# The end of an attention-and-density kernel: pacing of the last norm, early diagonals, order of the last units, a halved ending

## The chip, the cores and the metric

The kernel runs on one core of a Trainium2 chip. The core has a matrix engine (TensorE, PE in the profile, with its weight loads as PEld), a vector engine (VectorE, DVE), a scalar engine for activation functions (ScalarE, ACT), a general engine (GpSimd, POOL) and a queue for transfers (SyncE, SP). Each engine runs its own instructions in order and waits on semaphores for the others. The metric is the device time of one execution in microseconds (us). All data is float32.

## The reference

Two layers run one after the other on x of shape (8, 192, 64, 64). Cut to what matters:

```python
# layer 0: attention over the 4096 pixels of each image
x = x + L0(_gn(x))     # q, k: 24 channels, v: 192; out = softmax(q k) v
# layer 1: a density per value, with small per-channel matrices
def _logits_cumulative(logits, ms, bs, fs):         # filters 1, 3, 3, 3, 1
    for i in range(4):
        logits = einsum('cij,cjn->cin', softplus(ms[i]), logits) + bs[i]
        if i < 3:
            logits = logits + tanh(fs[i]) * tanh(logits)
    return logits
lower = _logits_cumulative(xr - 0.5, ms, bs, fs)    # xr = _gn(x)
upper = _logits_cumulative(xr + 0.5, ms, bs, fs)
sign = -sign(lower + upper)
likelihood = maximum(abs(sigmoid(sign * upper) - sigmoid(sign * lower)), 1e-06)
x = x + likelihood
```

`_gn` is a group norm over an image: a mean and a variance for each group of six channels. The density of an image can thus not start before the whole image has its attention result and the norm of that result is known.

## The kernel before, in words

The attention is one long stream of 1024 steps, 128 for each of the 8 images (`last = B * IMG`). A step multiplies queries and keys into scores (L769, PE), takes their exponential (L773, ACT) and multiplies it with the values (L784, PE). Row maxima for the softmax run 22 steps ahead (L697 on PE, L705 on DVE). Everything else is put between these by a small planner that works while the program is written, not while it runs.

The planner has two parts. `at(t, fn, cost, act, pe)` files a function under a step; `work_off(t, rate)` writes out what is due at that step, then starts a waiting PSUM job, then calls `density_step`. This second part deals out the density work of the image before: it gives each engine a credit per step (for DVE and PE the `rate`, for ACT 2.9 during the stream and the `rate` after it), and lets the oldest three units write out instructions while the credit lasts. A function that is filed with a cost takes its cost from the credit. So after the stream, where `t` no longer stands for a piece of attention, the `rate` says how many us of density work are written between two steps of anything else. It is 4.15.

A density unit is one of 12 pieces of an image: half c, channel group g, and s for lower or upper; its tiles are 128 x 1024. It goes through three rows of three: a tanh of x (L994), a linear part of x (L1003), nine multiply-adds ("mix", L1026), then gates and further affine steps and additions (L1019 and L1009 on ACT, L1026 on DVE). A `Unit` of the last image other than its first one takes its first nine multiply-adds and the linear part to PE instead: three sums of four products with diagonal matrices (`product`, L967), one diagonal per coefficient; its tanh of a sum is L975 and its gate L985. There are eleven such units. When lower and upper of a piece are both done, `ending` adds them, takes two tanhs, subtracts, masks, takes the absolute value and adds to x, and stores the result by two transfers (L1202). After the stream this is the form `alone`, on DVE and ACT.

The diagonals lie in freed tiles of the values. `diagonals(g)` makes nine for a group by scaling an identity on ACT (L865); it is filed for the fifth to seventh step after the stream. `linear_diagonals` (L871) makes the three that need the last norm, for all three groups, then works out the offsets `lower2` on DVE (L877 to L883), and hands four PSUM tiles to the units (`banks`): the two accumulators `b`, and `sc_tail` and `mx_tail`.

The end of the last image's attention is a chain of planner steps: a reciprocal (L804), two evacuations on ACT (L808), six transposes on PE (L817), the residual addition (L826), three statistics (L427), an aggregate (L436), a group mean on PE (L441), differences (L447 to L451), a group variance on PE (L456), L462 and L463, a square root on ACT (L469), and the final small steps (L475 to L491), which write `wn` and `bn`, the scale and offsets of the norm. Each of these stands in a step of its own, some thirteen in all. Then `density(7)` adds the 12 units of the last image. When only two units are left, the one with more DVE work goes first.

Of the kernel before, what the change touches and what calls it, by code (L numbers as in the profile page):

```python
# [10 lines left out]
AF = mybir.ActivationFunctionType  # L11
ALU = mybir.AluOpType
# [5 lines left out]
def kernel(  # L18
# [40 lines left out]
    nc = tc.nc  # L59

    B, C, H, W = x.shape
    N = H * W
    CR = w1t.shape[1]
    F = 512
# [4 lines left out]
    R = C // 3  # L69
# [4 lines left out]
    last = B * IMG  # L74
# [95 lines left out]
    for s in range(2):  # L170
        p = slice(R * s, R * s + R)
# [684 lines left out]
    banks = deque()  # L856
    lower2 = mm.rearrange("p g n -> p (g n)")[:, 0:36].rearrange("p (s g i) -> p s g i", s=4, g=3)

    def diagonals(g):

        d = vtiles.pop(0).rearrange("p a b c -> p (a b c)")[:, 0 : 12 * 128]
        d = d.rearrange("p (k n) -> p k n", k=12)
        diag.append(d)
        for k in range(9):
            nc.scalar.activation(d[:, k, :], ident, AF.Copy, scale=lc[:, g, k : k + 1])  # L865

    def linear_diagonals(b):
        wn, bn = norms[b, 1]
        for g in range(3):
            for i in range(3):  # L870
                nc.scalar.activation(  # L871
                    diag[g][:, 9 + i, :], ident, AF.Copy, scale=wn[:, g, 1, i : i + 1]
                )

        for s in range(2):
            d, q = lower2[:, s], lower2[:, 2 + s]
            nc.vector.tensor_copy(d, cb[:, :, 6:9])  # L877
            for j in range(3):
                nc.vector.tensor_tensor(
                    q, wsp[:, :, 12 + j : 21 : 3],  # L880
                    bn[:, s, :, 1, j : j + 1].to_broadcast([128, 3, 3]), ALU.mult,
                )
                nc.vector.tensor_tensor(d, d, q, ALU.add)  # L883
        for t in (
            *turns, ps_sc.tile([128, 2, F], F32, tag="sc", name="sc_tail"),
            ps_mx.tile([128, 2, F], F32, tag="mx", name="mx_tail"),
        ):
            banks.append(t)
# [186 lines left out]
    def density_step(t, rate):  # L1075
        if units and t < last:

            left = sum(len(u.todo["DVE"]) for u in units if u.key[0] == units[0].key[0])
            rate = left * COST["DVE"] / max(1, (units[0].key[0] + 2) * IMG + 15 - t) + OTHER
        act = ACT_RATE if t < last else rate  # L1080

        for eng, most in (("DVE", rate), ("ACT", act)):
            more = (rate if eng == "DVE" else 0.0) if t >= last else 1.3
            credit[eng] = min(credit[eng] + most, most + more)
        credit["PE"] = min(credit["PE"] + rate, rate)
        for eng in ("ACT", "PE", "DVE"):
            order = list(range(min(3, len(units))))
            if len(units) == 2:

                order.sort(key=lambda n: -len(units[n].todo["DVE"]))  # L1090
            for n in order:
                units[n].step(eng, t, list(units)[:n])
        for u in [u for u in units if not u.todo["DVE"]]:
            units.remove(u)

    def density(b):
        if b == B - 1:
            linear_diagonals(b)
# [25 lines left out]
    def ending(b, c, g):  # L1124


        z = [zs.pop((b, c, g, i)) for i in range(2)]
        halves = [slice(h * F, h * F + F) for h in range(2)]
        cell = {}

        def later(n, fn, *cost):
            at(now[0] + n, fn, *cost)

        def begin():
            if not bufs:
                later(1, begin)
                return
            endings.pop()
            cell["s"] = bufs.pop(0)
            if now[0] < last - 12:  # L1140
                for h in range(2):
                    pieces.append(lambda h=h: total(h))
            else:
                alone()

        def total(h):
            n = halves[h]
            later(1, lambda: tanhs(h), 0.0, 2.0)
            return nc.gpsimd.tensor_tensor(cell["s"][:, n], z[0][:, n], z[1][:, n], ALU.add)  # L1149

        def tanhs(h):
            for i in range(2):
                nc.scalar.activation(z[i][:, halves[h]], z[i][:, halves[h]], AF.Tanh, scale=0.5)
            s = cell["s"][:, halves[h]]
            nc.scalar.activation(s, s, AF.Sign)
            pieces.append(lambda: difference(h))
            pieces.append(lambda: masked(h))

        def difference(h):
            n = halves[h]  # L1160
            return nc.gpsimd.tensor_tensor(z[0][:, n], z[1][:, n], z[0][:, n], ALU.subtract)  # L1161

        def masked(h):
            n = halves[h]
            if h == 1:
                later(1, lambda: bufs.extend((cell["s"], z[1])))
                later(1, size, 0.0, 1.1)
                later(2, store, 1.3)
            return nc.gpsimd.tensor_tensor(z[0][:, n], z[0][:, n], cell["s"][:, n], ALU.mult)  # L1169

        def alone():

            s = cell["s"]

            def first():
                nc.vector.tensor_tensor(s, z[0], z[1], ALU.add)
                later(1, second, 0.0, 2.1)

            def second():
                for i in range(2):  # L1180
                    nc.scalar.activation(z[i], z[i], AF.Tanh, scale=0.5)
                later(1, third, 2.5)

            def third():
                nc.vector.tensor_tensor(z[0], z[1], z[0], ALU.subtract)
                nc.vector.scalar_tensor_tensor(z[0], s, 0.0, z[0], ALU.not_equal, ALU.mult)
                bufs.extend((s, z[1]))
                later(1, size, 0.0, 1.1)
                later(2, store, 1.3)

            later(1, first, 1.25)

        def size():
            nc.scalar.activation(z[0], z[0], AF.Abs, scale=0.5)

        def store():
            x_ = xc[b, c][:, g, :]
            nc.vector.scalar_tensor_tensor(x_, z[0], 1e-6, x_, ALU.max, ALU.add)
            bufs.append(z[0])
            for i in range(2):  # L1200
                k = i * N // 2 + c * 2 * F
                nc.sync.dma_start(  # L1202
                    out=ov[b, :, g, k : k + 2 * F], in_=x_[R * i : R * i + R]
                )
# [55 lines left out]
    def prepare(b, t):  # L1260
        seen = []

        def then():
            seen.append(0)
            if len(seen) == NP:
                norm_end((b, 0), 2 * NP, now[0] + 1, lambda: weights(b, normed))

        def normed():
            for i, c in enumerate(ORDER):
                for h in range(2):  # L1270
                    what = "kv" if i < 2 else "k"
                    use(b, 2 * c + h, what, max(now[0], t + 30 + 6 * (2 * i + h)), 1, 0, i < 2)

            for h in range(2):
                use(b, h, "q", t + 92, 0, 1, 0, t + 97)

        for d in range(NP):
            look(b, d, t + 1 + d, then)

        for i in (2, 3):  # L1280
            for h in range(2):
                use(b, 2 * ORDER[i] + h, "v", t + 100 + 4 * i + 2 * h, 0, 0, 1, t + 107 + 4 * i)
        for h in range(2):
            use(b, 2 + h, "q", t + 122, 0, 1, 0, t + IMG)
# [86 lines left out]
    for g in range(3):  # L1371
# [5 lines left out]

# [36 lines left out]
```

## Time and profile before

| What | Value |
|---|---|
| Median of 3 runs | 4918.28 us (4916.8 to 4919.44) |
| Profiled execution | 4916.79 us, span 4915.0 us |
| PE busy | 4740.1 us, 96% of the span |
| DVE busy | 4312.6 us, 88% |
| ACT busy | 3194.5 us, 65% |
| POOL busy | 514.0 us, 10% |
| Mean granted TensorE clock | 0.987 |
| Last attention matmul of the stream ends | about 4552 us |
| Norm results of the last image (L488) | 4603.25 us |
| First matmul of a PE unit that reads a tanh | 4615.66 us |
| Last matmul of a PE unit ends | about 4878.6 us |
| Last store instruction ends | about 4910.3 us |

The span runs from the first to the last instruction; the execution's own time is 1.79 us more. Times of single instructions below are counted from the span's start. A row of the order of time merges equal instructions that follow each other: its second number is their busy time together, and the number in brackets is the time for which the engine was idle before it, with the engine and line that ended the wait. The recorded duration of a DVE or ACT instruction overlaps the next one's by about 0.1 us. A matmul of a PE unit is two rows of 512 columns.

### The profile page before, as it was taken

To read this page: it belongs to the slowest core of one execution; us is meant where nothing else is said; L and a number is where in the kernel's file an instruction comes from. 1 tells how busy PE (TensorE), PEld (TensorE's weight loads), DVE (VectorE), ACT (ScalarE), POOL (GpSimd) and SP (SyncE) were. 2 spreads that over 40 slices of the span, in tenths; PEclk is the share of its full clock that TensorE was granted. 3 is DMA by queue.
4 is the path that set the end of the run, shared out by engine and by line. 5 is a ranking of instruction groups with operands and counts; after the bars stand their busy time and mean duration, and the time that the engine had idled before them with its cause. 6 is when DMAs were issued, how large, how long until landed. Compare 5 with 4: busy or idle time off the path is not lost.

```text
span 4915.0 us, 69887 instructions
## 1 busy us (share of the span) xinstructions
PE 4740.1 (96%) x29152; PEld 3505.3 (71%) x29152; DVE 4312.6 (88%) x4442; ACT 3194.5 (65%) x3709; POOL 514.0 (10%) x506
## 2 busy tenths in 40 slices
PE   7999999999999999999999999999999999999496
PEld 5777777777777777777777777777777777777232
DVE  5433359999999999999999999999999999998987
ACT  2333347776767766776776767776767767676765
POOL 0000001111011110210111200111111111111000
PEclk9999999999999999999999999999999999999798
DMA  2000020111200111010110111011111101000000
GB/s 56 26 22 18 14 52 4 32 28 31 51 18 18 42 37 34 23 37 24 42 30 21 32 40 40 18 31 32 31 34 32 28 22 28 11 22 5 9 13 13
DMA packets 111953, 135.49 MB, mean 28 GB/s; under 512 B 14738, under 2 KB 93076, under 8 KB 111636
## 3 DMA queue, kind: packets, MB, share of 16 engines
q1 hardware_dynamic: 110432, 130.65, 10.9%
q8 instruction: 228, 3.74, 0.3%
q14 instruction: 89, 0.73, 0.1%
q10 hardware_dynamic: 1204, 0.37, 0.0%
HBM read 105.82 MB, written 25.17 MB: 27 GB/s over the span
## 4 chain that ended last, share of the span: by engine, by line
PE 78%; DVE 16%; ACT 4%; issue 1%; POOL 1%; DMA 0%; ACTq 0%; SPq 0%; DVEq 0%; POOLq 0%
PE b L784 46%; PE sc L769 18%; DVE d L1026 10%; DVE rm L705 4%; PE b L658 4%; PE b L967 2%; PE b L630 2%; PE b L601 1%; PE sc_tail L967 1%; PE mx_tail L967 1%; PE mx L697 1%; PE b L817 1%; ACT d L1019 1%; ACT d L1009 1%; ACT e L773 1%
## 5 line engine op out<-in xcount | busy, mean ns | idle before, releaser
L784 PEld LDWEIGHTS b<-v,e 128*128 128x128 f32 x16384 | 2655.1, 190 | 777.0 <-issue 772.5
L784 PE MATMUL b<-v,e 128*128 128x193 f32 x16384 | 2958.9, 334 | 0.0
L773 ACT ACTIVATE e<-sc 128x1024 f32<-128x1024 f32 x1024 | 1046.7, 1022 | 1456.3 <-PE mx L697 1414.0
L705 DVE TENSOR_REDUCE rm<-mx 128x1 f32<-128x1024 f32 x1002 | 1223.3, 1221 | 459.6 <-PE mx L697 454.2
L769 PE MATMUL sc<-q,k 25*128 25x512 f32 x4096 | 1155.2, 640 | 16.8 <-ACT e L773 16.4
L697 PE MATMUL mx<-k,q 24*128 24x512 f32 x4008 | 1130.4, 640 | 4.9 <-DVE rm L705 4.9
L1026 DVE SCALAR_TENSOR_TENSOR d<-d,wsp,d 128x1024 f32<-128x1024 f32 x768 | 988.0, 1288 | 44.3 <-ACT d L1019 33.6
L1026 DVE SCALAR_TENSOR_TENSOR d<-d,lc,d 128x1024 f32<-128x1024 f32 x765 | 981.6, 1291 | 18.1 <-ACT d L1003 5.1
L1026 DVE SCALAR_TENSOR_TENSOR d<-d,tf,d 128x1024 f32<-128x1024 f32 x543 | 683.9, 1280 | 3.5 <-ACT d L1009 3.4
L1009 ACT ACTIVATE d<-d 128x1024 f32<-128x1024 f32 x543 | 569.6, 1055 | 57.1 <-DVE d L1026 55.7
L769 PEld LDWEIGHTS sc<-q,k 25*128 25x128 f32 x4096 | 306.2, 182 | 250.2 <-issue 195.8
L1114 POOL MEMSET pause<- 128x1 f32 x240 | 23.7, 99 | 3965.9 <-DVE d L1026 3965.9
L1019 ACT ACTIVATE d<-d,cb,wsp 128x1024 f32<-128x1024 f32 x351 | 433.3, 1235 | 0.8 <-DVE d L1026 0.2
L994 ACT ACTIVATE d<-xc,bn,wn 128x1024 f32<-128x1024 f32 x288 | 354.1, 1236 | 2.8 <-DVE bn L491 2.0
L1003 ACT ACTIVATE d<-xc,bn,wn 128x1024 f32<-128x1024 f32 x255 | 315.7, 1238 | 0.0
L697 PEld LDWEIGHTS mx<-k,q 24*128 24x128 f32 x4008 | 299.6, 182 | 16.9 <-DVE rm L705 13.5
L1149 POOL TENSOR_TENSOR d<-d,d 128x512 f32<-128x512 f32 x80 | 169.5, 2119 | 0.2
L1161 POOL TENSOR_TENSOR d<-d,d 128x512 f32<-128x512 f32 x80 | 167.7, 2097 | 0.0
L1169 POOL TENSOR_TENSOR d<-d,d 128x512 f32<-128x512 f32 x80 | 156.4, 1955 | 2.3 <-POOL pause L1114 0.6
L658 PE MATMUL b<-wv,xi 64*128 64x192 f32 x1344 | 139.5, 340 | 1.4 <-ACT pra L585 1.4
L658 PEld LDWEIGHTS b<-wv,xi 64*128 64x128 f32 x1344 | 106.5, 186 | 26.9 <-issue 20.9
L967 PE MATMUL b<-d,v 128*128 128x512 f32 x204 | 95.2, 618 | 17.0 <-ACT d L994 17.0
(171 smaller groups left out, 2373.5 us busy)
## 6 DMA issues: line engine op xcount, KB each, us to landing
xi<-in_x_dram SPq DMA_DIRECT2D x392, 192.0 KB, 3.4
xc<-in_x_dram SPq DMA_DIRECT2D x64, 384.0 KB, 8.0
out_dram<-xc SPq DMA_DIRECT2D x96, 256.0 KB, 3.2
d<-in_x_dram SPq DMA_DIRECT2D x16, 192.0 KB, 4.0
d<-in_wat_dram ACTq DMA_DIRECT2D x2, 144.0 KB
cb<-in_den_b_dram SPq DMA_DIRECT2D x6, 2.2 KB, 2.1
ff<-in_den_f_dram SPq DMA_DIRECT2D x6, 2.2 KB, 2.2
bq<-in_b_dram ACTq DMA_DIRECT2D x4, 0.1 KB
```

Of the source, the lines that this page charges most:

```text
L658: nc.tensor.matmul(pv[:, s, 0:C], lhsT=t[p, g, k * 128 : k * 128 + 128] if g < 3 else one_row[p], rhs=wf["v", b][p, g, :] if g < 3 else wf ...
L697: nc.tensor.matmul(sc[:, s, :], lhsT=tile_of(qt[b, n // 2], n, j)[r], rhs=kt[b][r, u : u + F], start=True, stop=True,)
L705: nc.vector.tensor_reduce(out=rowmax[b, n][:, j, k : k + 1], in_=sc, axis=AX.XY, op=ALU.max)
L769: nc.tensor.matmul(sc[:, s, :], lhsT=kt[b][r, k : k + 128], rhs=qt[b, n // 2][r, :, u : u + 256], start=True, stop=True,)
L773: return lambda: nc.scalar.activation(e, sc, AF.Exp)
L784: nc.tensor.matmul(a[:, j, 0 : C + 1], lhsT=e[:, s, j * 128 : j * 128 + 128], rhs=v[:, s, p % 4, :], start=p == 0 and s == 0 and j % 2 == ...
L967: nc.tensor.matmul(out[:, h, :], lhsT=diag[g][:, 3 * i + n - 1 if n else 9 + i, :], rhs=src[:, h * F : h * F + F], start=n == 0, stop=n == 3,)
L994: nc.scalar.activation(self.buf[k], self.src(), AF.Tanh, bias=bn[:, s, g, 0, i : i + 1], scale=wn[:, g, 0, i : i + 1],)
L1003: nc.scalar.activation(self.buf[k], self.src(), AF.Identity, bias=bn[:, s, g, 1, i : i + 1], scale=wn[:, g, 1, i : i + 1],)
L1009: nc.scalar.activation(self.buf[k], self.buf["l", k[1], k[2]], AF.Tanh)
L1019: nc.scalar.activation(self.buf[k], self.buf["l", n - 1, 0], AF.Identity, bias=offset, scale=wsp[:, g, w : w + 1],)
L1026: nc.vector.scalar_tensor_tensor(dst, src, factor, dst, ALU.mult, ALU.add)
```

## The change

Four things change, all behind or near the end of the stream.

- After the stream the `rate` is 1.3 instead of 4.15 until the last norm's results are there, and 4.15 from then on. Fewer density instructions are written between the steps of the norm's chain.
- The 27 diagonals that don't need the norm are made during the last image, one per planner step, at steps 93 to 101, 104 to 112 and 117 to 125 of its 128. Each is filed with 0.4 of ACT.
- The three diagonals that need the norm are made at once for group 0, three steps later for group 1 and six steps later for group 2. The offsets and the hand-over of the PSUM tiles (`tail`) come one step later than the norm, with a DVE cost of 2.2.
- After the stream the last two units keep their order, older first. The very last ending is written in two halves of 512 columns, with four transfers instead of two.

```diff
-    def diagonals(g):
+    def diagonals(g, t):
+        def one(k):
+            if k == 0:
+                d = vtiles.pop(0).rearrange("p a b c -> p (a b c)")[:, 0 : 12 * 128]
+                diag.append(d.rearrange("p (k n) -> p k n", k=12))
+            nc.scalar.activation(diag[g][:, k, :], ident, AF.Copy, scale=lc[:, g, k : k + 1])
-        d = vtiles.pop(0).rearrange("p a b c -> p (a b c)")[:, 0 : 12 * 128]
-        d = d.rearrange("p (k n) -> p k n", k=12)
-        diag.append(d)
         for k in range(9):
-            nc.scalar.activation(d[:, k, :], ident, AF.Copy, scale=lc[:, g, k : k + 1])
+            at(t + k, lambda k=k: one(k), 0.0, 0.4)
...
-            if len(units) == 2:
+            if len(units) == 2 and t < last:
                 order.sort(key=lambda n: -len(units[n].todo["DVE"]))
...
         if b == B - 1:
-            linear_diagonals(b)
+            linear_diagonals(b, 0)
+            for g in (1, 2):
+                at(now[0] + 3 * g, lambda g=g: linear_diagonals(b, g), 0.0, 1.2)
+            at(now[0] + 1, lambda: tail(b), 2.2)
...
             s = cell["s"]
+            parts = halves if (b, c, g) == (B - 1, 1, 2) else [slice(0, 2 * F)]
             def first():
-                nc.vector.tensor_tensor(s, z[0], z[1], ALU.add)
+                for n in parts:
+                    nc.vector.tensor_tensor(s[:, n], z[0][:, n], z[1][:, n], ALU.add)
                 later(1, second, 0.0, 2.1)
             def second():
+                for n in parts:
+                    for i in range(2):
+                        nc.scalar.activation(z[i][:, n], z[i][:, n], AF.Tanh, scale=0.5)
...
+            for n in parts:
+                x_ = xc[b, c][:, g, n]
+                nc.vector.scalar_tensor_tensor(x_, z[0][:, n], 1e-6, x_, ALU.max, ALU.add)
                 for i in range(2):
...
+                        out=ov[b, :, g, k + n.start : k + n.stop], in_=x_[R * i : R * i + R]
...
             if b + 1 < B:
                 prepare(b + 1, t)
+            else:
+                diagonals(0, t + 93)
+                diagonals(1, t + 104)
+                diagonals(2, last - 11)
...
-    for g in range(3):
-        at(t + 4 + g, lambda g=g: diagonals(g))
     while due or units or jobs or loads:
-        work_off(t, RATE)
+        work_off(t, RATE if (B - 1, 1) in norms else 1.3)
         t += 1
```

More of the change, by code (lines that the diff above doesn't have):

```diff
@@ L857, with linear_diagonals, tail @@
     lower2 = mm.rearrange("p g n -> p (g n)")[:, 0:36].rearrange("p (s g i) -> p s g i", s=4, g=3)
-    def diagonals(g):
-        d = vtiles.pop(0).rearrange("p a b c -> p (a b c)")[:, 0 : 12 * 128]
-        d = d.rearrange("p (k n) -> p k n", k=12)
-        diag.append(d)
+    def diagonals(g, t):
[4 more added lines that the diff above has]
+            nc.scalar.activation(diag[g][:, k, :], ident, AF.Copy, scale=lc[:, g, k : k + 1])
         for k in range(9):
-            nc.scalar.activation(d[:, k, :], ident, AF.Copy, scale=lc[:, g, k : k + 1])
-    def linear_diagonals(b):
+            at(t + k, lambda k=k: one(k), 0.0, 0.4)
+    def linear_diagonals(b, g):
         wn, bn = norms[b, 1]
-        for g in range(3):
[L870 to L873, printed above, removed]
+        for i in range(3):
+            nc.scalar.activation(
+                diag[g][:, 9 + i, :], ident, AF.Copy, scale=wn[:, g, 1, i : i + 1]
+            )
+    def tail(b):
+        wn, bn = norms[b, 1]
         for s in range(2):
@@ L1173, in alone @@
             s = cell["s"]
+            parts = halves if (b, c, g) == (B - 1, 1, 2) else [slice(0, 2 * F)]
             def first():
-                nc.vector.tensor_tensor(s, z[0], z[1], ALU.add)
+                for n in parts:
+                    nc.vector.tensor_tensor(s[:, n], z[0][:, n], z[1][:, n], ALU.add)
                 later(1, second, 0.0, 2.1)
             def second():
-                for i in range(2):
-                    nc.scalar.activation(z[i], z[i], AF.Tanh, scale=0.5)
+                for n in parts:
+                    for i in range(2):
+                        nc.scalar.activation(z[i][:, n], z[i][:, n], AF.Tanh, scale=0.5)
@@ L1182, in second @@
                 later(1, third, 2.5)
             def third():
-                nc.vector.tensor_tensor(z[0], z[1], z[0], ALU.subtract)
-                nc.vector.scalar_tensor_tensor(z[0], s, 0.0, z[0], ALU.not_equal, ALU.mult)
+                for n in parts:
+                    y = z[0][:, n]
+                    nc.vector.tensor_tensor(y, z[1][:, n], y, ALU.subtract)
+                    nc.vector.scalar_tensor_tensor(y, s[:, n], 0.0, y, ALU.not_equal, ALU.mult)
                 bufs.extend((s, z[1]))
-                later(1, size, 0.0, 1.1)
@@ L1189, in third, with size @@
-                later(2, store, 1.3)
+                later(1, lambda: size(parts), 0.0, 1.1)
+                later(2, lambda: store(parts), 1.3)
             later(1, first, 1.25)
[L1193 to L1198, printed above, removed]
-            bufs.append(z[0])
[L1200 to L1204, printed above, removed]
+        def size(parts=(slice(0, 2 * F),)):
+            for n in parts:
+                nc.scalar.activation(z[0][:, n], z[0][:, n], AF.Abs, scale=0.5)
@@ L1205, in store @@
+        def store(parts=(slice(0, 2 * F),)):
+            for n in parts:
+                x_ = xc[b, c][:, g, n]
+                nc.vector.scalar_tensor_tensor(x_, z[0][:, n], 1e-6, x_, ALU.max, ALU.add)
+                for i in range(2):
+                    k = i * N // 2 + c * 2 * F
+                    nc.sync.dma_start(
+                        out=ov[b, :, g, k + n.start : k + n.stop], in_=x_[R * i : R * i + R]
+                    )
+            bufs.append(z[0])
             if g == 2:
@@ L1370 @@
     homes[:] = [(turns[1], [0, 0])]
-    for g in range(3):
-        at(t + 4 + g, lambda g=g: diagonals(g))
     while due or units or jobs or loads:
-        work_off(t, RATE)
+        work_off(t, RATE if (B - 1, 1) in norms else 1.3)
         t += 1
```

## The prediction

> **What bounds the kernel now.** I read the stage table first, then each engine's instructions in order of time, then the waits. The table below gives five stretches: start:end and length, then busy time with the instruction count for PE, PEld, DVE, ACT and POOL, the granted TensorE clock, and the DMA share.
>
> ```profile
> 4400.00:4551.00 151.00, 150.51 (x852) 113.46 (x851) 136.00 (x123) 107.57 (x113) 14.01 (x13) 1.00 0.08 18
> 4551.00:4604.00 53.00, 3.67 (x17) 2.80 (x15) 51.08 (x62) 34.58 (x58) 0.00 (x0) 0.56 0.04 10
> 4604.00:4716.00 112.00, 87.39 (x183) 37.23 (x184) 90.42 (x85) 74.65 (x75) 0.00 (x0) 0.87 0.04 10
> 4716.00:4871.00 155.00, 142.58 (x329) 61.74 (x328) 132.24 (x108) 104.99 (x98) 0.00 (x0) 1.00 0.04 10
> 4871.00:4915.00 44.00, 7.63 (x18) 3.04 (x16) 30.75 (x25) 18.20 (x17) 0.00 (x0) 0.62 0.09 24
> ```
>
> The stream ends near 4552. In it PE is the bound (150.51 of 151). In the next 53 us PE does almost nothing while DVE is full (51.08): DVE works on image 6's last units, with the last norm's small steps between them. From 4616 the PE units run; in their settled part (third stretch from the end to 4871) PE is busy 92%. The last 44 us are one unit's DVE and ACT chain.
>
> ```profile
> 4569.10 0.95 DVE L826 TENSOR_TENSOR xc<-xc,b 128x768 f32<-128x768 f32 x1
> 4603.25 0.23 DVE L488 TENSOR_SCALAR wn<-wx,nrm 128x18 f32<-128x18 f32 x1
> 4615.66 6.88 PE L967 MATMUL b<-d,v 128*128 128x512 f32 x12 [7.91 <-ACT d L994]
> 4639.80 1.98 PE L967 MATMUL mx_tail<-d,v 128*128 128x512 f32 x4 [1.81 <-ACT d L994]
> 4652.85 5.34 PE L967 MATMUL mx_tail<-d,v 128*128 128x512 f32 x8 [11.06 <-ACT d L994]
> ...
> 4698.07 8.34 PE L967 MATMUL b<-d,v 128*128 128x512 f32 x12 [3.83 <-ACT d L994]
> ...
> 4746.28 5.42 PE L967 MATMUL mx_tail<-d,v 128*128 128x512 f32 x12 [1.81 <-ACT d L994]
> ```
>
> Columns: start, busy, engine, line, operation, count; in brackets the idle time before it and who ended it. The norm's results (L488) come 51 us after the stream. The first PE unit starts at 4615.66; its successor waits 11.06 in the middle of a sum and the next 3.83, because the tanh inputs (L994) stand in ACT's queue behind DVE work. Later each unit waits only about 1.8.
>
> **The change, part by part.**
>
> *Short steps.* Between the reciprocal at 4551.97 and the norm's first reciprocal at 4602.20, DVE runs 37 wide instructions. In the new order there are 11: five before the residual, none up to the statistics' end, two, two and two between the three later small groups. I lay them out with the old rows: 1.20 between independent wide instructions, 1.31 when one needs its predecessor, 1.13 an ACT affine, 0.96 a tanh, 0.05 a handoff. The ending of image 6's unit waits once for its absolute value on ACT, so the residual starts at 4560.9 (was 4569.10), the aggregate ends at 4563.4, the mean is read at 4565.9, the variance at 4569.5, the norm's reciprocal starts at 4572.1. The norm is 30.1 us earlier.
>
> But the 26 displaced instructions do not vanish. The planner lets only the oldest three units step, so image 6's last two units and the one non-PE unit of image 7 go ahead of the first PE unit. Between the lower2 work and the first PE gate DVE now has 47 wide instructions (was 16). From 4575.9, 33 at 1.20 and 14 dependent ones at 1.31 give 58; with one 0.7 us wait for an ACT affine and 1.2 for another, the first gate comes at 4635.7, later than the old 4629.24. The first PE unit's tanh inputs stand behind the 33rd of these: they finish at 4619.8, 4621.0 and 4625.75, so PE starts 4.1 us later than 4615.66. So the early norm alone gains nothing at this point: at about 4616 DVE has done the same number of instructions in both orders, since it was nearly full.
>
> What it gains comes after. The non-PE unit is then further along, and PE's 11.06 and 3.83 waits fall away. First sum done 4628.0 (third input, two matmuls of it, 0.5 for a slow start); then ten sums at 6.87 and three unit waits of 1.75 put the eleventh at 4702.0. In the old trace the eleventh sum ends at 4713.3. Lead: 11.3. From about the eleventh gate the DVE order is the old one, and ACT's nearly so, so the lead carries on: the settled cycle (45.3 per two units) is unchanged.
>
> A wait of 3.83 before 4698.07 was followed by 12 matmuls in 8.34 instead of 5.42: 2.9 lost at half clock, part of what is saved. The Trainium skill ("TensorE: Matmul & The Clock Gate", What's actually happening) has the half clock return after an idle window of about 3.4 us. The 1.8 rows show no slowing. Here the page speaks against the change in one place: PE is now idle from 4559 and starts with three broken-up inputs. By the page 3.4 us of work at half rate would cost 1.7; the wait for the third input covers all but about 0.5, which I take. By the row of the old start (6.88 for 12, against 5.16 at the 0.43 pace) it would also be 1.7: range 0 to 1.7.
>
> *Diagonals in the stream.* 27 ACT copies leave the gap for the last image, one a step.
>
> ```profile
> 4424.12 1.00 ACT L773 ACTIVATE e<-sc 128x1024 f32<-128x1024 f32 x1
> 4519.52 1.02 ACT L773 ACTIVATE e<-sc 128x1024 f32<-128x1024 f32 x1 [2.84 <-PE sc L769]
> 4565.65 7.99 ACT L865 ACTIVATE v<-ident,lc 128x128 f32<-128x128 f32 x27
> 4595.89 1.28 ACT L469 ACT_TABLE_LOAD   x1
> 4597.18 0.20 ACT L469 ACTIVATE sq<-ve 128x1 f32<-128x1 f32 x1
> ```
>
> Each costs 0.30 (7.99/27). In most steps ACT idles 0.6 to 2.8 before the next exponential and hides it. In about two of the 27 steps ACT is already late (no idle, as at 4424.12) and queued behind the copy is the exponential, then the attention matmuls. Bounds: 0, and 27 x 0.30 = 8.0 if every step passed it on. I take two steps, 0.5. In the gap their removal saves nothing, since DVE was the bound there.
>
> *Table loads.* Two stay, before the square root and before the next tanh, but the second now stands before image 6's tanh. The Trainium skill ("ScalarE: Activation LUTs", What ACT_TABLE_LOAD costs) charges 1.28 plus a drain of 1.38 for each switch. Here the row has 1.28 and the square root starts 0.01 after it; I charge 1.3. By the page the norm and the queue behind it would come 1.4 to 2.8 later, and the first PE unit no more than that.
>
> *Lower2 one step later, diagonals of groups 1 and 2 later:* 0.9 of ACT work each, hidden, as the first sum needs only group 0 and DVE sets the pace; uncovered it would be 1.8.
>
> *The end.* With two units left the order no longer favours the younger, so the older finishes its last three gates and sums before the last sum's gate.
>
> ```profile
> 4873.32 5.31 PE L967 MATMUL b<-d,v 128*128 128x512 f32 x12
> ...
> 4899.58 2.60 DVE L1026 SCALAR_TENSOR_TENSOR d<-d,wsp,d 128x1024 f32<-128x1024 f32 x2
> 4902.21 1.22 DVE L1176 TENSOR_TENSOR d<-d,d 128x1024 f32<-128x1024 f32 x1
> 4903.47 2.00 ACT L1181 ACTIVATE d<-d 128x1024 f32<-128x1024 f32 x2 [4.92 <-DVE d L1176]
> 4905.51 1.23 DVE L1185 TENSOR_TENSOR d<-d,d 128x1024 f32<-128x1024 f32 x1 [2.07 <-ACT d L1181]
> 4906.77 1.22 DVE L1186 SCALAR_TENSOR_TENSOR d<-d,d 128x1024 f32<-128x1024 f32 x1
> 4908.02 1.06 ACT L1194 ACTIVATE d<-d 128x1024 f32<-128x1024 f32 x1 [2.55 <-DVE d L1186]
> 4909.11 1.23 DVE L1198 SCALAR_TENSOR_TENSOR xc<-d,xc 128x1024 f32<-128x1024 f32 x1 [1.12 <-ACT d L1194]
> ```
>
> PE's last sum ends at 4878.6. Old: the unit's last addition ends 23.6 later, the final store instruction 31.7 later. New, from the same zero: last gate 2.8 (DVE still has the older unit's sums), additions for the three rows from 4.0, 8.8 and 13.7, three gates, last addition ends 22.4. Halves: about 0.65 for each DVE half and 0.62 an ACT half (the row of L1153); pipelined, the last store instruction ends at 28.4 instead of 31.7. Gain 3.3: 1.2 from the order, 2.1 from the halves. SP issues four transfers of 128 KB (0.53 each) for two of 256 KB (3.2 to landing): the second pair queues 0.3 behind the first, and half the bytes return about as much. Zero.
>
> *Sum:* 11.3 + 3.3 - 0.5 = 14.1. The profiled execution took 4916.79 (span 4915.0 and 1.79 around it), so 4902.7. The median of the runs shown is 1.49 above it: 4904.2, rounded to 4904.
>
> **Rivals.**
> 1. *It only moves work.* The early norm is filled up with image 6's work, and PE's waits reappear behind the queue at other places. For: DVE's equal progress at 4616. Against: the two long waits came while a fresh non-PE unit ran beside PE, and less of it is left. Then only the tail counts: 4918.3 - 3.3 = 4915.
> 2. *The copies stall the stream.* PE has no slack there. 7.5 more than I charge: 4911.5. Against: the idle before most exponentials.
> 3. *Better:* DVE idles less than I let it and PE's lead reaches 18 instead of 11.3: 4897.
> 4. *Slower: the clock falls between units.* Should the tanh inputs of each unit come 3.6 us late or more instead of 1.8, PE would restart at half clock: 1.8 + 2.9 = 4.7 a unit. Ten units follow the first: 47, so 4951. It takes three units to eat the 14, and from the sixth on the kernel is slower by over 0.2%. For: the row at 4698.07. Against: the settled order is unchanged and shows 1.8.
>
> **How the numbers follow.** Forecast 0.70 (its own range 4899 to 4909), rival 1 0.13, rival 2 0.07, rival 3 0.05, rival 4 0.05. A measurement tells 0.2%, or 9.8 us, from no change: faster is below 4908.4. Of the forecast's 0.70, 0.05 lies above that. Faster 0.65 + 0.05 = 0.70; same 0.05 + 0.13 + 0.07 = 0.25; slower 0.05. The range 4898 to 4915 reaches to rival 1 and leaves out rivals 3 and 4 and the far edge of the forecast's own.
>
> **What would show it.** Right: wn at about 4573, first tanh-fed matmul at about 4620, no PE wait over 3 us after the first sum, the eleventh sum near 4702, PE's last sum near 4868, no copies in the gap, the last addition about 22 after PE's end. Wrong: PE waits over 3 between units, a stream that ends later than 4553, or a first PE unit later than 4625.

## The result and the profile after

The changed kernel takes 4905.18 us (median of 7 runs, 4901.24 to 4907.48) against 4918.28 (4916.8 to 4919.51) for the kernel before: a ratio of 0.9972, with a 95% interval of 0.9961 to 0.9984. The forecast was 4904.

The stage table of the changed kernel, with the columns of the one before and the stretches cut at the same kind of place:

```profile
4400.00:4551.00 151.00, 150.51 (x852) 112.46 (x850) 135.35 (x123) 112.21 (x137) 17.26 (x15) 1.00 0.08 18
4551.00:4604.00 53.00, 11.76 (x48) 8.50 (x46) 48.51 (x70) 35.92 (x43) 0.00 (x0) 0.63 0.04 10
4604.00:4716.00 112.00, 85.83 (x192) 36.95 (x192) 101.75 (x84) 72.20 (x67) 0.00 (x0) 0.89 0.04 10
4716.00:4861.00 145.00, 132.60 (x306) 57.56 (x307) 125.15 (x103) 101.72 (x95) 0.00 (x0) 1.00 0.04 11
4861.00:4906.00 45.00, 11.75 (x28) 4.94 (x26) 34.20 (x32) 19.63 (x22) 0.00 (x0) 0.66 0.10 23
```

The first stretch has 24 more ACT instructions than before, and PE is still busy for 150.51 of 151. In the gap DVE still sets the pace. In the settled part (fourth row) PE is busy for 91%, against 92% before. So the change has not altered what bounds any stretch. It has shortened the way from the gap into the settled part, and the end.

Next, single rows of the changed kernel in order of time: the reciprocal behind the stream, the norm's result, then PE's first sum and one of the waits that follow it, with the first gate between them, and PE's last sum.

```profile
4556.87 0.17 DVE L804 RECIPROCAL rc<-b 128x4 f32<-128x4 f32 x1
4577.76 0.23 DVE L488 TENSOR_SCALAR wn<-wx,nrm 128x18 f32<-128x18 f32 x1
4624.80 7.78 PE L972 MATMUL b<-d,v 128*128 128x512 f32 x12 [42.80 <-ACT d L999]
4640.65 1.27 DVE L990 SCALAR_TENSOR_TENSOR d<-d,tf,b 128x1024 f32<-128x1024 f32 x1
4649.77 5.42 PE L972 MATMUL mx_tail<-d,v 128*128 128x512 f32 x12 [1.75 <-ACT d L999]
...
4867.44 5.31 PE L972 MATMUL b<-d,v 128*128 128x512 f32 x12
```

The old waits of 11.06 and 3.83 are gone, and with them the slow row of 8.34 us (granted clock 0.65). What is left are ten waits of 1.75 to 1.81 (between 4649.77 and the last unit), each followed by 12 matmuls at full rate.

And the tail of the changed kernel, DVE only:

```profile
4892.51 2.60 DVE L1031 SCALAR_TENSOR_TENSOR d<-d,wsp,d 128x1024 f32<-128x1024 f32 x2
4895.15 1.29 DVE L1186 TENSOR_TENSOR d<-d,d 128x512 f32<-128x512 f32 x2
4897.06 0.69 DVE L1198 TENSOR_TENSOR d<-d,d 128x512 f32<-128x512 f32 x1 [0.61 <-ACT d L1192]
...
4899.72 1.47 DVE L1213 SCALAR_TENSOR_TENSOR xc<-d,xc 128x512 f32<-128x512 f32 x2
```

The "last store instruction" of the tables is DVE's last addition to x (L1198 before, L1213 now); the transfers follow it. From the unit's last addition (L1031, 4895.11) to its end (4901.19) it takes 6.1 us, where it was 8.1.

**One disturbance before reading on.** This profiled execution was behind the old one from its first 110 us on: the reciprocal L804 starts at 4556.87 instead of 4551.97. One window of the changed kernel's head, with the columns of the stage table, shows such a place:

```profile
100.00:104.00 4.00, 3.18 (x12) 1.68 (x13) 1.00 (x1) 1.79 (x2) 0.00 (x0) 0.50 0.02 4
```

The same window of the kernel before:

```profile
100.00:104.00 4.00, 4.00 (x27) 3.01 (x26) 1.23 (x1) 1.03 (x1) 0.00 (x0) 1.00 0.00 0
```

The changed kernel ran here at a lower granted clock, in a part of the program that the change does not touch. So I count all places behind the stream from the start of L804, and a second profile of the same kernel (below) tells whether the lag belongs to it. Counted this way:

| Place, us after L804 starts | before | forecast | after |
|---|---|---|---|
| norm results (L488) | +51.28 | +21.0 | +20.89 |
| first matmul that reads a tanh | +63.69 | +67.8 | +67.93 |
| first sum done | +70.6 | +76.0 | +75.7 |
| first PE gate | +77.3 | +83.7 | +83.8 |
| eleventh sum done | +161.3 | +150.0 | +150.5 |
| PE's last sum done | +326.7 | +316 | +315.9 |
| last store instruction done | +358.4 | +344.4 | +344.3 |

Sum by sum, PE is 5.1 us behind the old kernel at its first three sums, then 7.9 ahead, then 5.8, and 10.8 ahead from the tenth sum to the last.

Counted from L804 the gain is 14.1 us. That is not yet the forecast's 14.1: the forecast took off 0.5 for the copies in the stream, which lie ahead of L804, so from there on it had 11.3 + 3.3 = 14.6. (The last two forecasts of the table carry these 0.5; without them they are +315.4 and +343.8.) And L804 itself is no longer quite the end of the stream:

```profile
4546.43 5.50 PE L784 MATMUL b<-v,e 128*128 128x193 f32 x32
4551.97 0.18 DVE L804 RECIPROCAL rc<-b 128x4 f32<-128x4 f32 x1
```

is the kernel before, and

```profile
4551.03 5.50 PE L784 MATMUL b<-v,e 128*128 128x193 f32 x32
```

with the L804 above the changed one. The reciprocal starts 0.05 us after the last attention matmul there and 0.34 after it here, because DVE is still busy. From the end of the stream on PE, the gain is therefore 13.8.

### The profile page after: what moved, and what is told of

Same layout as the page of the kernel before. It is cut to its first block, busy times and chain, and to the rows that moved or that the text cites. A ratio compares the mean times of both kernels' runs of the same rounds, so it can differ in the third digit from the quotient of the medians.

```text
span 4905.7 us, 69892 instructions
## 1 busy us (share of the span) xinstructions
PE 4741.1 (97%) x29152; PEld 3507.0 (71%) x29152; DVE 4312.5 (88%) x4446; ACT 3193.5 (65%) x3712; POOL 514.1 (10%) x506
## 4 chain that ended last, share of the span: by engine, by line
PE 77%; DVE 17%; ACT 4%; issue 1%; POOL 1%; DMA 0%; SPq 0%; ACTq 0%; DVEq 0%; POOLq 0%
PE b L784 46%; PE sc L769 17%; DVE d L1031 11%; DVE rm L705 4%; PE b L658 4%; PE b L972 2%; PE b L630 2%; PE b L601 1%; PE sc_tail L972 1%; PE mx_tail L972 1%; PE mx L697 1%; PE b L817 1%; ACT d L1024 1%; ACT d L1014 1%; ACT e L773 1%
## 5 line engine op out<-in xcount | busy, mean ns | idle before, releaser
L1031 DVE SCALAR_TENSOR_TENSOR d<-d,wsp,d 128x1024 f32<-128x1024 f32 x768 | 987.2, 1287 | 50.6 <-ACT d L1024 40.0
L1031 DVE SCALAR_TENSOR_TENSOR d<-d,lc,d 128x1024 f32<-128x1024 f32 x765 | 981.1, 1290 | 14.7 <-ACT d L1008 2.4
L1031 DVE SCALAR_TENSOR_TENSOR d<-d,tf,d 128x1024 f32<-128x1024 f32 x543 | 683.4, 1279 | 2.7 <-ACT d L1014 2.6
L1008 ACT ACTIVATE d<-xc,bn,wn 128x1024 f32<-128x1024 f32 x255 | 315.4, 1237 | 0.0
```

The source lines that it names most:

```text
L1008: nc.scalar.activation(self.buf[k], self.src(), AF.Identity, bias=bn[:, s, g, 1, i : i + 1], scale=wn[:, g, 1, i : i + 1],)
L1031: nc.vector.scalar_tensor_tensor(dst, src, factor, dst, ALU.mult, ALU.add)
```

## The experiments

### The parts alone

First, each part put alone into the kernel before. The short steps:

```diff
-        work_off(t, RATE)
+        work_off(t, RATE if (B - 1, 1) in norms else 1.3)
```

> Short steps alone: the kernel before with only the rate of 1.3 until the last norm; diagonals in the gap, order and ending as before. My theory (the early norm gains nothing by itself; the gain comes from PE's later waits, which fall away): norm results about 29 us earlier than before, counted from the end of the stream (the 8 us of copies now lie in a shorter gap, cost up to 1), first PE unit not earlier than before, PE waits of 11 and 3.8 gone, PE's last sum about 10 us earlier; 4908. Rival 'only moves work': PE waits reappear elsewhere, 4918. Rival 'the early norm is the gain': first PE unit up to 29 earlier, 4890.

Measured: 4908.02 (4906.38 to 4912.6), ratio 0.9982 (0.9975 to 0.9988). PE's matmuls on tanhs and the norm's result in this kernel, in order of time:

```profile
4575.53 0.23 DVE L488 TENSOR_SCALAR wn<-wx,nrm 128x18 f32<-128x18 f32 x1
4611.48 3.51 PE L967 MATMUL b<-d,v 128*128 128x512 f32 x4 [31.45 <-ACT d L994]
...
4647.41 6.03 PE L967 MATMUL mx_tail<-d,v 128*128 128x512 f32 x8 [7.95 <-ACT d L994]
4784.22 7.11 PE L967 MATMUL b<-d,v 128*128 128x512 f32 x12 [2.08 <-ACT d L994]
```

The norm comes at +20.8, as in the full change. But PE starts at +56.8, 11 us earlier than there, and then waits 7.95 inside a sum. The last sum ends at +318.3, 8.4 before the old kernel's and 2.4 after the changed one's. Its last store instruction comes 31.7 after that sum, as before. In this pair an earlier start of PE's units does not bring an earlier end.

The diagonals alone, in the stream, with the other parts undone:

```diff
-    for g in range(3):
-        at(t + 4 + g, lambda g=g: diagonals(g))
...
+                diagonals(0, t + 93)
+                diagonals(1, t + 104)
+                diagonals(2, last - 11)
```

> Early diagonals alone: 27 copies during the last image, all else as before. My theory: the copies are hidden by ACT's idle time in the stream and were hidden behind DVE in the gap: 4917.5 to 4918.3, no step of the stream longer. Rival 'the copies stall the stream': up to 8 longer, 4926. Rival 'the copies in the gap were the cost': 8 shorter, 4910.

Measured: 4917.51 (4915.62 to 4920.7), ratio 1.0002 (0.9994 to 1.001). Its PE rows have the old waits:

```profile
4657.31 6.12 PE L972 MATMUL mx_tail<-d,v 128*128 128x512 f32 x8 [11.06 <-ACT d L999]
4703.31 7.03 PE L972 MATMUL b<-d,v 128*128 128x512 f32 x12 [3.82 <-ACT d L999]
```

The copies save nothing in the gap, and the median shows no cost in the stream. The changed kernel's exponentials agree: those of the last image ran 4.65 us behind the old ones at the first copies (4424.05) and 4.61 at the stream's end (4551.21), so the 27 copies held up no exponential that the trace can show. But the last copy (4548.26) pushes back a tanh and a linear part behind it in ACT's order, and DVE's last instructions ahead of the reciprocal wait for these. L804 starts 0.34 or 0.35 us after the last attention matmul in all ten profiles with the early copies and 0.05 or 0.06 after it in the four without: 0.3 us, what one copy takes.

The order of the last units and the halves alone:

```diff
-            if len(units) == 2:
+            if len(units) == 2 and t < last:
...
+            parts = halves if (b, c, g) == (B - 1, 1, 2) else [slice(0, 2 * F)]
```

> The end alone: older unit first when two are left after the stream, and the last ending in halves; rate and diagonals as before. My theory: from PE's last sum to the last store instruction 28.4 instead of 31.7; 4915. The order of two units also holds while image 6's last two units are worked off in the gap, which I had not put in the sum: taken as 0. Rival (order of no consequence, halves cost as much as they save): 4918.

Measured: 4915.54 (4912.27 to 4919.11), ratio 0.9996 (0.9988 to 1.0004), which alone could be no change. PE's last sum and the last store instruction, then one row from the settled part:

```profile
4790.74 7.11 PE L979 MATMUL b<-d,v 128*128 128x512 f32 x12 [2.10 <-ACT d L1006]
...
4874.17 5.31 PE L979 MATMUL b<-d,v 128*128 128x512 f32 x12
...
4906.46 1.47 DVE L1219 SCALAR_TENSOR_TENSOR xc<-d,xc 128x512 f32<-128x512 f32 x2
```

From the end of PE's last sum (4879.48) to that of the last store instruction (4907.93) it takes 28.45 us instead of 31.7, as worked out. Half of this gain is given back ahead of it: the last sum ends at +328.4 instead of +326.7, and one wait of 2.10 was followed by 12 matmuls in 7.11 instead of 5.42. The three parts alone move the median by 9.1, by nothing measurable and by 1.6, which may be none: the short steps carry most of the change. Added up they give 10.2 of the 13.1; the rest comes only with the parts together (see the order, below).

### Is it the start of PE or the amount of DVE work?

The changed kernel's PE units start 4 us later than the old ones and end 11 us earlier. If what counts is how many wide DVE instructions stand ahead of the settled part, an early PE unit buys nothing while the last image's one unit on DVE and ACT remains. So I swapped the first two units of the last image: PE's first unit comes before the other.

```diff
-                    units.append(Unit(b, c, g, s))
+                    first = b == B - 1 and c + g == 0
+                    units.append(Unit(b, c, g, 1 - s if first else s))
```

> The changed kernel with the first two units of the last image in the other order: the PE unit ahead of the one that runs without PE. First gate behind 18 wide DVE instructions instead of 48, but the first gate of the second PE unit is the 61st, as before. My theory (the wide DVE instructions count, not when PE starts): PE starts more than 30 earlier, waits as much between the first and the second PE unit, and the end stays: 4901 to 4909. Rival (PE's start decides): 4875.

Measured: 4911.19 (4908.98 to 4913.71), ratio 0.9988 (0.9981 to 0.9994), slower than the change and than the 4901 to 4909 that I expected. The PE rows of this kernel:

```profile
4583.25 7.00 PE L972 MATMUL b<-d,v 128*128 128x512 f32 x12 [6.71 <-ACT d L999]
4637.16 7.35 PE L972 MATMUL mx_tail<-d,v 128*128 128x512 f32 x12 [31.46 <-ACT d L999]
4669.40 8.29 PE L972 MATMUL sc_tail<-d,v 128*128 128x512 f32 x12 [9.44 <-ACT d L999]
4717.56 8.10 PE L972 MATMUL b<-d,v 128*128 128x512 f32 x12 [3.83 <-ACT d L999]
```

PE starts at +31.9, 36 us earlier than in the changed kernel, and ends its last sum 8 us later (+323.9). It waits 31.46, 9.44 and 3.83, and after each of these it runs slower: the granted clock was 0.74, 0.65 and 0.67 over the twelve matmuls. In this kernel the other unit stands behind the first PE unit, and DVE works on it while PE waits for the tanhs of the second: between 4580 and 4625 DVE is busy for 42.38 us and PE for 22.45. The rival's 4875 is far off.

The other side of it, all 12 units on PE, so that the 26 instructions of the one DVE unit fall away:

```diff
-            self.on_pe = b == B - 1 and c + g + s > 0
+            self.on_pe = b == B - 1
```

> The changed kernel with one thing more: the first unit of the last image also goes to PE (12 units on PE instead of 11), so that its 26 wide DVE instructions become 14 and it brings PE work at once. My theory (DVE's queue of 47 wide instructions ahead of the first PE gate is what holds PE): first gate behind 18 of them, first tanh-fed matmul about 4588 by the old count, one wait of about 8 before the second unit, then 32 sums at 6.87 and ten waits of 1.78: PE's last sum about 8 earlier than in the changed kernel, so 4893 to 4896. Rival (PE is the bound, 21 us more of it): 4915 to 4925.

Measured: 4900.81 (4898.56 to 4902.44), ratio 0.9965 (0.9953 to 0.9978). PE starts at +31.9 here too, with a wait of 9.88 before its second unit:

```profile
4586.65 7.43 PE L972 MATMUL b<-d,v 128*128 128x512 f32 x12 [6.54 <-ACT d L999]
4619.40 8.11 PE L972 MATMUL mx_tail<-d,v 128*128 128x512 f32 x12 [9.88 <-ACT d L999]
```

The last sum ends at +313.0, only 2.9 ahead of the changed kernel's, although a whole unit has left DVE; I had expected 8. Of the 36 us by which PE starts earlier, three more sums take 20.6, the wait of 9.88 comes on top, and the slow row behind it takes 2.7. From 4644.71 on it has ten waits of 1.75 to 1.81, 17.8 us in all, as many as the changed kernel.

Pacing the steps before the norm still lower:

```diff
-        work_off(t, RATE if (B - 1, 1) in norms else 1.3)
+        work_off(t, RATE if (B - 1, 1) in norms else 0.1)
```

> The changed kernel with a rate of 0.1 instead of 1.3 until the last norm: three wide DVE instructions stand in the norm's chain instead of eleven. My theory: the norm comes a few us earlier still (about 16 after the stream instead of 21), but DVE then idles about 8 in the gap instead of 3, and that is lost: 4907 to 4911. Rival (the earlier the norm the better): 4898 to 4901.

Measured: 4906.64 (4905.2 to 4910.15), ratio 0.9978 (0.9971 to 0.9985). The norm comes at +13.0, 8 us earlier than in the change, yet PE's first sum starts later (+69.2):

```profile
4567.06 0.23 DVE L488 TENSOR_SCALAR wn<-wx,nrm 128x18 f32<-128x18 f32 x1
4623.22 7.05 PE L972 MATMUL b<-d,v 128*128 128x512 f32 x12 [51.65 <-ACT d L999]
4649.61 7.11 PE L972 MATMUL mx_tail<-d,v 128*128 128x512 f32 x12 [3.89 <-ACT d L999]
```

The end comes at +348.6 instead of +344.3. My reason for a loss was wrong: DVE idles 4.2 us in the gap instead of 3.4, not 8. The 4.3 us are the start (1.3 later), a wait of 3.89 where the changed kernel has 1.75, and the 7.11 behind it instead of 5.42, less 0.7 in the first sum. The norm 8 us earlier did not help here.

### The last two terms of the sum

The change without the new order of the last two units:

```diff
-            if len(units) == 2 and t < last:
+            if len(units) == 2:
```

> The changed kernel without the new order of the last two units (younger first again); halves, early diagonals and short steps stay. The order also acts on image 6's last two units in the gap. My theory: from PE's last sum to the last store about 29.6 instead of 28.4 and the start as with the short steps alone (PE earlier, a wait of about 8 later): PE's last sum within 2 of the changed kernel's; 4905 to 4908. Rival (the order is what pays at the start): 4912.

Measured: 4908.35 (4904.46 to 4909.58), ratio 0.998 (0.9972 to 0.9988). From PE's last sum to the last store instruction it takes 29.6 us, 1.2 more than with the order, as worked out. But the trace shows a second effect of the same flag. It also acts in the gap, where image 6 is down to its last two units. Without it PE starts at +56.5, then waits 1.33, 1.81 and 7.95 and later 2.08 with a slow row of 7.11, which are the rows of the short steps alone; the last sum ends at +318.1 instead of +315.9. So the order is worth 1.2 behind the last sum and 2.3 ahead of it, of which 1.7 is the slow row. I had booked only the first by name; the second stands inside the 11.3 that I had worked out for the lead.

The change without the halves:

```diff
-            parts = halves if (b, c, g) == (B - 1, 1, 2) else [slice(0, 2 * F)]
+            parts = [slice(0, 2 * F)]
```

> The changed kernel with the last ending in one piece. Theory: the halves are worth 2.1 us behind PE's last sum; last store instruction ends 30.5 us after PE's last sum instead of 28.4; time 4907.3. Rival: the halves gain nothing since each half instruction has its own overhead and handoff: 4905.

Measured: 4905.07 (4903.15 to 4907.93), against 4902.82 for the changed kernel beside it. PE's last sum and the last store instruction of this kernel:

```profile
4862.29 5.31 PE L972 MATMUL b<-d,v 128*128 128x512 f32 x12
...
4896.90 1.23 DVE L1213 SCALAR_TENSOR_TENSOR xc<-d,xc 128x1024 f32<-128x1024 f32 x1 [1.12 <-ACT d L1208]
```

4867.60 to 4898.13 is 30.53 us, 2.1 more than with the halves: the term was right. (The 4907.3 that I expected stood on the first set of runs, where the kernel before took 4918.28 and not 4915.94.)

### The changed kernel once more

> The changed kernel once more, unchanged. Theory: the 4.6 us by which its first profile was behind the old one when the stream ended is a property of that execution (half-clock stretches in the first 110 us), so the stream's reciprocal (L804) starts anywhere from 4551 to 4557 and the distances after it repeat within 1 us: norm +20.9, first tanh-fed matmul +67.9, PE's last sum +315.9, last store instruction +344.3. Rival: the lag belongs to the changed kernel: the reciprocal starts at 4556 to 4557 again. Time 4905.

Measured: 4902.82 (median of 8 runs, 4900.88 to 4905.72), ratio 0.9972 (0.9961 to 0.9982). Its rows:

```profile
4550.97 0.17 DVE L804 RECIPROCAL rc<-b 128x4 f32<-128x4 f32 x1
...
4618.89 7.91 PE L972 MATMUL b<-d,v 128*128 128x512 f32 x12 [42.57 <-ACT d L999]
...
4861.66 5.31 PE L972 MATMUL b<-d,v 128*128 128x512 f32 x12
...
4893.94 1.47 DVE L1213 SCALAR_TENSOR_TENSOR xc<-d,xc 128x512 f32<-128x512 f32 x2
```

The reciprocal is at 4550.97, so the lag of the first profile was a property of that execution. Behind it the distances repeat: norm +20.89, first tanh-fed matmul +67.92, last sum +316.0, last store instruction +344.4.

### The waits of 1.8 us

The forecast took the settled cycle with its waits of about 1.8 per unit as given. The planner's rule says where they may come from: an instruction that makes a new tile is written only while

```python
if makes and len(bufs) <= sum(u.need() for u in older) + len(endings):
    return
```

does not hold. A younger unit's tanh inputs are written late in ACT's order when the buffers that are left are reserved for older units. Behind the stream other tiles lie unused. So the units got seven more buffers when the last norm is known: three tiles of the values, two of the exponentials and two of the queries' tag (the kernels differ in nothing else).

```diff
     def tail(b):
         wn, bn = norms[b, 1]
+        for v in vtiles:
+            bufs.append(v.rearrange("p a b c -> p (a b c)")[:, 0 : 2 * F])
+        vtiles.clear()
+        for tag in ("e", "q"):
+            for i in range(2):
+                x_ = work.tile([128, 2, F], F32, tag=tag, bufs=2, name=f"x{tag}{i}")
+                bufs.append(x_.rearrange("p a b -> p (a b)"))
```

On the kernel with all 12 units on PE:

> All twelve units of the last image on PE, and seven more buffers for density units once the last norm is there (three tiles of the values, two of the exponentials, two of the queries, all free by then). With them the planner writes some tanh inputs of the next unit ahead of the instruction that waits for the last sum. My theory (the waits of 1.75 to 1.81 at each unit come from ACT's order: the next unit's tanh inputs stand behind the wait for the last sum): eleven waits of 1.78 mostly vanish, 15 to 20 off the 4901 of the kernel without the buffers, so 4882 to 4887; DVE, at 39 of 45 us, still fits into 41.2. Rival (DVE or its handoffs set the cycle): the waits move, 4898 to 4902.

Measured: 4871.91 (4869.8 to 4874.21), ratio 0.9908 (0.9894 to 0.9923), better than expected. A window of its settled part:

```profile
4715.00:4760.00 45.00, 45.00 (x106) 19.89 (x106) 44.65 (x37) 34.16 (x33) 0.00 (x0) 1.00 0.05 12
```

Its last matmuls and its last store instruction:

```profile
4828.56 1.88 PE L979 MATMUL mx_tail<-v,v 128*128 128x512 f32 x4
...
4862.01 1.47 DVE L1220 SCALAR_TENSOR_TENSOR xc<-d,xc 128x512 f32<-128x512 f32 x2
```

PE is full (45.00 of 45), and DVE nearly so (44.65). The last sum ends at +279.6, 33.4 earlier than without the buffers. 17.8 of these are the ten waits. Most of the rest is the start, where the first tanh-fed matmul comes at +26.8 and no wait above 3.1 follows. DVE is now further behind when PE ends, so the tail takes 33.0 instead of 28.4.

Is the twelfth unit on PE needed for this? On the changed kernel with its eleven:

> The changed kernel (eleven PE units, one unit on DVE and ACT) with seven more buffers handed to the units when the last norm is known. Theory: the waits of about 1.8 us between PE units come from ACT instructions that stand behind a buffer still in use; the buffers remove most of them, and DVE, which is 26 wide instructions behind because of the non-PE unit, becomes the bound. From the kernel with twelve PE units, which took 4900.8 without and 4871.9 with the buffers, a gain of 15 to 25 us over the changed kernel: 4880 to 4890, with the first tanh-fed matmul still near +68 us after the stream's reciprocal. Rival: the buffers pay only where all twelve units run on PE, because otherwise DVE sets the pace: 4898 to 4906.

Measured: 4876.86 (4876.29 to 4880.36), ratio 0.992 (0.9906 to 0.9935). PE's rows:

```profile
4588.26 8.08 PE L979 MATMUL b<-d,v 128*128 128x512 f32 x12 [12.12 <-ACT d L1006]
4626.71 7.63 PE L979 MATMUL mx_tail<-d,v 128*128 128x512 f32 x12 [14.92 <-ACT d L1006]
```

26 us better than the changed kernel beside it, where I expected 15 to 25. One thing I had wrong: the first tanh-fed matmul is at +37.5 and not near +68, since the buffers also let the first PE unit's inputs be written before the older units are done. PE then waits 14.92, once, and afterwards 0.61, 1.81 and 0.64.

And on the kernel before, with nothing else of the change:

> The kernel before with the same seven buffers and nothing else of the change. Theory (buffers, not the short steps, hold back the settled part): the waits of 1.8 us go, the waits of 11.06 and 3.83 shrink: 4890 to 4900. Rival (in the old order the norm is late and DVE's queue, not a buffer, sets each wait): 4912 to 4918.

Measured: 4890.25 (4888.9 to 4892.62), ratio 0.9947 (0.9932 to 0.9962). Its PE waits from the first sum on:

```profile
4614.12 6.94 PE L974 MATMUL b<-d,v 128*128 128x512 f32 x12 [7.90 <-ACT d L1001]
4660.94 3.17 PE L974 MATMUL sc_tail<-xe,v 128*128 128x512 f32 x4 [3.83 <-ACT xe L1001]
4666.79 1.98 PE L974 MATMUL sc_tail<-xe,v 128*128 128x512 f32 x4 [0.45 <-ACT xe L1001]
```

After the last of these there is none: from 4716 to 4847 PE is busy for the whole 131 us. The wait of 11.06 is gone as well, although PE starts where it did (+63.7), and the 3.83 shown is another one: it stands at +110.5, the old one stood at +146.1. So the long waits of the old kernel, too, hung on buffers and not on the late norm alone. Whether fewer than seven would do was not tried. The two gains add up in number: the buffers are worth 25.7 on the kernel before and 26.0 on the changed one, the change 13.1 without them and 13.4 with them. But with the buffers the change works in another way. The waits that it took out of the old kernel are gone already; here it starts PE 26.2 us earlier (+37.5 against +63.7), of which 10.3 are left at the last sum (+286.6 against +296.8), and the end brings 2.1. That the sums agree is chance as far as these runs tell.

## Why the prediction was right

*Short steps.* Right at every place of the table above, within 0.5 us: the norm 30 us earlier, the first PE unit 4 us later all the same, the first gate later than the old one. The instruction counts hold too: 11 wide DVE instructions up to the norm, and 47 between the offsets and the first gate. The lead came out at 10.8 and not 11.3. The reason held that the displaced DVE instructions come back ahead of PE: without more buffers, four kernels start PE 11 to 36 us earlier than the change, and three of them end its last sum later.

Why the old long waits vanish was told only in part. "The non-PE unit is further along" is right, and the swap of the first two units shows the reverse: with that unit late, waits of 31.46, 9.44 and 3.83 come. But what lets a late unit hold back PE is, by the planner's rule, that buffers are reserved for it, and the runs with more buffers bear this out: with seven more, the old order has only a 3.83 and a 0.45 left.

*The half-clock start.* I took 0.5 of 0 to 1.7. The first sum ended at +75.7 against +76.0. Its first two inputs were worked on at half clock up to 4629.4 and done at 4630.6, just as the third tanh was (4630.5), and the rest ran at full clock. So the low end was right: the third input ended it, not the clock.

*Diagonals in the stream.* 0.5 taken, 0.3 found, and by another way than I had it. I had two copies pass through the exponential to the attention matmuls; no exponential came later. One copy passes through ACT and DVE to the reciprocal. ACT's idle time hid the others.

*Table loads.* The load takes 1.28 and what follows starts 0.01 after it, in the changed kernel too:

```profile
4573.81 1.28 ACT L469 ACT_TABLE_LOAD   x1
4575.10 0.20 ACT L469 ACTIVATE sq<-ve 128x1 f32<-128x1 f32 x1
```

No drain of 1.38 as in the Trainium skill ("ScalarE: Activation LUTs", What ACT_TABLE_LOAD costs) shows on either side of the load, which starts 0.02 after the ACT instruction ahead of it has ended. The norm came 0.1 ahead of the time that I had with 1.3, so the page's larger price would have made that step worse.

*The end.* 28.4 from the last sum to the last store instruction, as forecast. Its two terms were shown apart, 1.2 by the order and 2.1 by the halves.

*The sum.* 14.1 forecast. Between the two profiles, from the end of the stream on PE: 10.8 for the lead, less 0.3 for the copies, and 3.3 for the end, 13.8. The lead was 0.5 too large and the copies 0.2 too dear, so the errors partly cancel. The medians moved by 13.1 in both sets of runs (the second from 4915.94 to 4902.82). That the first median fell within 1.2 of 4904 is in part luck: medians of the same kernel in different sets of runs lie up to 2.4 apart.

*The rivals.* That it only moves work (4915) is what the end alone gives (4915.54); the short steps alone took 9.1 off, so it fell. The copies did not stall the stream. The lead stayed at 10.8 and not at the 18 of rival 3. Rival 4 needed PE waits of 3.6 and more in each unit; they stayed at 1.8.

What the prediction did not see, since it asked only about the change, is that those waits of 1.8 were worth more than the change: it treated the settled cycle as fixed. The version with all twelve units on PE and seven more buffers is faster than both kernels, by 45 us than the one before.

## What to carry to other kernels

When an engine is full, taking work out of its way at one place puts the same work ahead of the next; count its instructions to the place where the bound engine settles, not to the first one that starts earlier. A wait that returns in every cycle at the same size is worth asking about before a long wait that comes once: look for what keeps the waiting instruction from being written earlier in its queue, and free buffers are the first thing to try. Count two profiles from a common event near the change, because a difference of a few us may have arisen long before it; and check that the change does not move that event.

## What was not expected of the hardware

TensorE fell to half clock after waits that are shorter than I had thought. The 3.83 of the old kernel was followed by 8.34 us for 12 matmuls, and I set the limit for rival 4 there. But 2.08 and 2.10 were followed by 7.11 (short steps alone, the end alone), while 1.75 to 1.81 never had an effect, and neither did a wait of 3.09 in the kernel with twelve units and more buffers (5.42).

The clock that the traces record tells why. In all 14 profiles it is either 1.00 or 0.50, and the points at which it changes lie whole multiples of 3.41 us apart; where they lie differs from execution to execution. Cut at these points, the wait of 2.08 falls into one stretch (busy time of PE is the second number, the clock the third from the end):

```profile
4781.84:4785.25 3.41, 1.33 (x4) 0.55 (x4) 3.37 (x4) 3.41 (x5) 0.00 (x0) 1.00 0.22 79
4785.25:4788.66 3.41, 3.41 (x6) 1.35 (x5) 1.62 (x2) 2.90 (x4) 0.00 (x0) 0.50 0.00 0
```

The wait of 3.09 is shared by two:

```profile
4617.37:4620.78 3.41, 1.76 (x5) 0.45 (x3) 3.41 (x4) 3.27 (x4) 0.00 (x0) 1.00 0.00 0
4620.78:4624.20 3.42, 1.98 (x5) 1.02 (x6) 3.38 (x4) 3.42 (x4) 0.00 (x0) 1.00 0.01 2
4624.20:4627.61 3.41, 3.41 (x10) 1.50 (x9) 3.38 (x4) 0.24 (x1) 0.00 (x0) 1.00 0.00 0
```

So what counts is how long PE idles within one such stretch, not how long the wait is. From the end of the stream to PE's last matmul, over all 14 profiles, 50 stretches at full clock were followed by one at half clock, and PE was idle in each of them for 2.02 us or more; 990 were followed by full clock, and PE was idle in none of them for more than 1.97. Back to full clock it went after 43 stretches with at most 0.66 us idle, and not after 218 with 0.73 or more. An estimate of the two limits from these numbers is 2.0 and 0.7 us of 3.41. They hold for this part of the kernel alone: in the head and in the stream, with other matmuls, the clock also fell after stretches with less idle time.

The Trainium skill ("TensorE: Matmul & The Clock Gate", What's actually happening) says that the clock is decided in windows of about 3.4 us that run freely, so that the same wait can fall well or badly. The traces agree. It asks for an idle window, though, and here PE was busy for up to 1.39 of the 3.41 us ahead of a fall.

A fall that lasted one stretch cost 1.7 us (7.11 instead of 5.42), one that lasted two cost 2.9 (8.34). In the head, the same wait of 2.25 before the first attention matmuls was followed by 16 matmuls in 2.88 in the kernel before and in 4.78 in the changed kernel's first profile, which came out of its head, with longer stretches at a low clock, about 5 us late: a third of what the change brings.
